# A sandwich of attention layers: transposing by halves of the array's rows

## The chip, the core and the metric

The kernel runs on one core of one Trainium2 chip. The metric is the time of one execution on the device in microseconds (us), the median of several runs. The core's engines work side by side, each through its own queue in order: PE (TensorE) multiplies matrices, PEld is PE's loading of the stationary operand, DVE (VectorE), ACT (ScalarE) and POOL (GpSimd) work elementwise, SP issues most of the DMAs. PE writes only to PSUM, which has eight banks of 512 float32 per partition here; ACT and DVE take its results from there to SBUF.

## The reference

The input x is 4 x 2048 x 256 in float32. First comes attention over all tokens, then two layers of local attention and feed-forward:

```python
x = x + _layernorm(_L0_attn_ref(_layernorm(x, axis=-1)), axis=-1)
x = x + _layernorm(_L0_ffn_ref(_layernorm(x, axis=-1), wqkv, q_scale, k_scale, wo, ln_g, ln_b, w1, b1, w2, b2), axis=-1)
```

`_L0_attn_ref` takes the scores x xᵀ, a softmax over their second axis and the product with x. One layer of `_L0_ffn_ref` (DEPTH = 2, 8 heads of 64, windows of 128 tokens) is

```python
h = shift_token(x); q, k, v = split(h @ wqkv)
q, k = rotary_xpos(l2norm(q) * qs, l2norm(k) * ksc)
o = local_attention(q, k, v)        # a window sees itself and the window before it, at most 128 tokens back
x = x + o @ wo
h = layernorm(shift_token(x)) * lg + lb
a, g = split(h @ w1 + b1)           # hidden width 682
x = x + (a * gelu(g)) @ w2 + b2
```

## The kernel before

Tokens lie on the partitions for row statistics and the residual stream, features lie there for products. Every operand of a product is kept in two float32r parts (`Split`: `hi`, the rounded value, and `lo`, the rest), and `products` (L149) makes three matmuls of each product: lo with hi, hi with lo, hi with hi. `split` (L132, L137) makes the parts from a PSUM bank: ACT copies it into `hi`, then DVE subtracts `hi` from the bank into `lo`. So each bank that is split stays taken until DVE has finished, and DVE waits for ACT.

The program has two phases. `global_phase` does the attention over all tokens for the four batch elements. `layer_phase` then walks over 128 steps (2 layers x 4 batch elements x 16 windows of 128 tokens). A step runs four generators in turns that are written out by hand in `TURNS`: `q` is `queries_keys` for the window two steps ahead, `s` the softmax of the next window, `v` (`outputs`) the attention output of this window, and `f` the feed-forward of two windows at a time. The order in which a generator's stages are called sets priorities; the framework's planner then orders the instructions of each engine by these and by its own estimate of when operands are ready, so neighbours on PE can come from different stages.

The places that the change touches, by the names under which the profile shows them:

- `queries_keys` makes q and k of a window in `qk` (tokens on the partitions, 16 heads x 64). After rotation (L616, L623, L645) and the scaling of k (L648) it transposes eight 128 x 128 blocks (L657): four of q into one bank `pqkT`, which is split into `qT`, then four of k into the next `pqkT`, split into `kT`.
- `similarities` takes the products `sim` of kT and qT. A head has 64 features, so the two heads of a pair use 64 of the array's 128 rows each, and write to two banks. DVE adds the mask and reduces (L702), ACT takes the exponential (L707), `pr` holds the weights, and POOL or ACT normalizes them (L720, L718).
- `weights(m)` transposes the weights of head pair m: four 128 x 128 blocks (two windows of keys x two heads; two blocks in a batch element's first window), L730, into one bank `pp`, which is split into `pT`.
- `values(m)` multiplies values and `pT` into `po`; two pairs share a bank, which is split into `oT`; `pw` is the product with wo. In the order of stages: weights(0), weights(1), values(0), weights(2), values(1), weights(3), values(2), and so on.
- The feed-forward has `phn` (transposes of the normalized rows), `pa` (first product) and `pf` (second product); `ph` are the transposes of h, `pv` the values, `pqk` the products for q and k.
- `BANKS` says how many banks each kind of PSUM tile has and which kinds share them: sim, pa, phn and pv share two; po and pw three; pf, ph and pqk one; pqkT one; pp one. `PLEFT` names those on the left side of PSUM, which come when the global phase gives up its big banks; the others come when that phase is over (`pools.more(2)`).
- `FIRST` orders the first steps of the layers into the end of the global phase: `q` and `r` are queries and keys of the first two windows, `c` a step of the global phase's ending, `s` the first window's softmax.

Steps that make a transpose are `nc.tensor.transpose(out, block, ident)`: the block is the stationary operand (PEld's row), the identity is what moves (PE's row, 128 columns).

Of the kernel before, what the change touches and what calls it, by code (L numbers as in the profile page):

```python
# [8 lines left out]
F32 = mybir.dt.float32  # L9
# [5 lines left out]
P = 128  # L15
HEADS = 8
DH = 64
# [11 lines left out]
BANKS = {'sim': (2, ('sim', 'pa', 'phn', 'pv')), 'po': (3, ('po', 'pw')), 't75': (1, ('pf', 'ph', 'pqk')), 't551': (1, ('pqkT',)), 't378': (1, ('pp', 'pb'))}  # L29
# [3 lines left out]
PLEFT = ('sim', 't75', 't551')  # L33
FIRST = 'qqccqrrccqrqqrccrrssss'
# [12 lines left out]
class Split:  # L47
    """A float32 operand in two float32r parts whose sum is exact: its upper 12 bits and the rest."""
# [9 lines left out]
def sandwich_kernel(  # L58
# [16 lines left out]
    """x += LN(attention over the batch's tokens of LN(x)); x += LN(two local-attention layers of LN(x)).  # L75

    First the attention over all tokens for each batch element, then each layer for all of them,
    with that layer's weights in SBUF. Tokens are on the partitions for the row statistics and the
    residual stream, features for the products, which are taken of operands in two parts each.
    """  # L80
    nc = tc.nc
# [3 lines left out]
    HID = w2.shape[1]  # L85
# [3 lines left out]
    NC = HID // P  # whole chunks of the hidden layer  # L89
    TAIL = HID - NC * P  # and the rest, the gate's at partition 64  # L90
    GT = 64
    # Where rows of the tail lie again: to, from, how many.
    PIECES = ((TAIL + 1, 0, GT - TAIL - 1), (GT + TAIL, GT - TAIL - 1, P - 1 - GT - TAIL))
    RING = 3  # windows whose keys and values are kept
# [6 lines left out]
    # ---------------------------------------------------------------- constants  # L101
# [8 lines left out]
    # Query i of a window sees keys i .. i + 128 of the previous and its own window: those of the  # L110
    # previous from i on, those of its own up to i. Here for the order previous, own, previous.
# [12 lines left out]
    # ---------------------------------------------------------------- operands in two parts  # L124
# [17 lines left out]
    def products(dst, terms, whole=()):  # L142
        """dst = the sum of the terms' lhsT.T @ rhs, with all of float32's bits, and of whole's as they are."""
        todo = []
        for a, b in terms:
            todo += [(a.lo, b.hi), (a.hi, b.lo), (a.hi, b.hi)]
        todo += whole
        for n, (a, b) in enumerate(todo):
            nc.tensor.matmul(dst, a, b, start=(n == 0), stop=(n == len(todo) - 1))  # L149

    # ---------------------------------------------------------------- row statistics
    def statistics(parts, n, name):
        """Mean and variance of n rows' parts, and 1/sqrt(variance + eps): [P, n, 2], [P, n]."""
# [18 lines left out]
    def normalize_all(dst, src, mv, rstd, engines, name):  # L172
        """Rows i of src, normalized, on the vector engine or the scalar engine."""
# [20 lines left out]
    def add_context(xg, y, b, g):  # L194
        """x + LN(y) goes to DRAM, and y becomes LN of that."""
# [10 lines left out]
    # ---------------------------------------------------------------- attention over all tokens  # L206
    JG = 2

    def global_phase(early, res, keep, big, bank):
        """Attention over all tokens.  # L210

        It stops before the last group's scores, when it's done with early, and after them, when
        it's done with res; the rest, in steps, uses only keep and bank.
        """
# [3 lines left out]
        def slot(tag, n, last):  # L218
            """The pool and the tag for the n-th of a kind of tiles; last are those that the last group uses."""
            n, last = n % GB[tag], [i % GB[tag] for i in last]  # L220
            return (res if n in last else early), f"{tag}{n}"

        def load_x(b, g):
            pool, tag = slot("x", b * NG + g, [B * NG - 1])
            t = pool.tile([P, 4, D], F32, tag=tag, bufs=1, name=f"x_{b}_{g}")
            # The first to come is waited for.
# [6 lines left out]
        def prepare(b, g):  # L233
            """LN(x) of 512 tokens with the features on the partitions."""
            xg = xt[b, g]
            mv, rstd = statistics([[xg[:, s, :]] for s in range(4)], 4, f"x_{b}_{g}")
            # |LN(x_j)|^2, the shift of column j's exponents: the exponents are 64 at most, one is 0.
# [21 lines left out]
        def scores(b, jg, hf):  # L259
            """exp of a half of the rows of JG chunks of scores."""  # L260
# [12 lines left out]
            for j in range(jg * JG, (jg + 1) * JG):  # L273
# [6 lines left out]
                # The scores are symmetric: those of the groups before are transposed here.  # L280
# [27 lines left out]
            for j in range(jg * JG, (jg + 1) * JG):  # L308
                # The sums belong to the contraction's index, so they divide LN(x).
# [14 lines left out]
        def context(b, jg, hf):  # L324
            """Adds the context of JG chunks; at the end x + LN(context) and LN of that go to DRAM."""
            for g in (2 * hf, 2 * hf + 1):
# [19 lines left out]
                if jg == NW // JG - 1:  # L346
                    if b + 1 < B:
                        add_context(early.tile([P, 4, D], F32, tag="xr", bufs=GB["xr"], name=f"xr_{b}_{g}"), y, b, g)
                    # The last one's rest is done when the first layer takes it.
# [37 lines left out]
    # ---------------------------------------------------------------- weights of a layer  # L387
# [5 lines left out]
    def tables(early, pool, l):  # L393
        """Rotation tables with the scales of q and k; the halves are swapped as the rotation does."""
# [29 lines left out]
    # The weights' parts, as they lie in SBUF.  # L424
# [11 lines left out]
    def split_weights(pool, bank, l):  # L436
        """Leaves layer l's weights in two parts in DRAM, piece by piece; each is left half a turn to arrive."""
        # The scale of the layer norm goes into w1, its shift into the bias.
# [34 lines left out]
        for i, (kind, ks, cols, src) in enumerate(pieces):  # L473
# [14 lines left out]
            # The lower part takes raw's place.  # L488
# [18 lines left out]
        # The tail's parts and the bias's, which meet rows of ones, share the rows of one product.  # L507
# [13 lines left out]
    def load_weights(pool, w, l, kinds):  # L521
        """Layer l's weights into w, as soon as the ones before aren't used any more."""
# [8 lines left out]
    # ---------------------------------------------------------------- the layers  # L531
    def layer_phase(pool, bank, ending):
# [22 lines left out]
        def features(l, b, u):  # L555
            """h of windows 2u and 2u + 1, features on the partitions: the second half comes one token late."""
# [21 lines left out]
        def queries_keys(l, b, w, n, wt, own):  # L578
            """Queries, keys and values of window w, left in own; in stages."""
# [19 lines left out]
            # Rotation, with the decay, the scales and, for q, the factor -8 in the tables; l2norm.  # L599
# [46 lines left out]
            # The similarities are scaled by q's.  # L646
# [6 lines left out]
            own["slot"] = n % RING  # L653
            for j, dst in enumerate((own["qT"], kT[:, n % RING])):
                pt = bank(f"pqkT_{at}_{j}")
                for c in range(4):
                    nc.tensor.transpose(  # L657
                        pt[:, c * P : (c + 1) * P],
                        qk[:, j * HEADS + 2 * c : j * HEADS + 2 * c + 2, :].rearrange("p h d -> p (h d)"),
                        ident,  # L660
                    )
                split(dst, pt.rearrange("p (c t) -> p c t", c=4))
                yield

        def local_attention(l, b, w, wt, before, own):
            """Window w sees itself and the window before it; y += its attention. In two streams of stages."""
# [5 lines left out]
            else:  # L672
# [3 lines left out]
                # In the order of their slots.  # L676
# [7 lines left out]
            def similarities(gq):  # L684
                # Negated similarities; the two heads of a pair use the two halves of the array's
                # rows, and so two banks.
# [37 lines left out]
            def weights(m):  # L724
                """The weights of pair m with the keys on the partitions."""
                pp = bank(f"pp_{at}_{m}").rearrange("p (f r t) -> p f r t", f=2, r=2)
# [330 lines left out]
```

## Time and profile before

| | |
|---|---|
| median of 3 runs | 3478.69 us (3476.59 to 3486.24) |
| profiled execution, span from first to last instruction | 3480.2 us |
| TensorE's mean granted clock | 0.991 |
| PE busy | 3374.0 us, 97% |
| PEld busy | 3069.6 us, 88% |
| DVE busy | 2932.9 us, 84% |
| ACT busy | 2495.6 us, 72% |
| POOL busy | 1933.8 us, 56% |
| transposes pp (L730) | 1984, busy 314.6 us |
| transposes pqkT (L657) | 1024, busy 158.9 us |
| similarities sim (L149) | 3 x 1024 matmuls of 64 rows, busy 788.2 us |

Of the profiled execution only the span is recorded; it stands 1.5 us from the median of the runs, so sums against the span and against the median are the same to 0.05%. PE's rows overlap: a matmul's row is longer than the time after which the next one starts, so PE's cost is read from the distance of starts, in PE's rows and above all in PEld's (a load that isn't held up starts when the matmul before it starts to stream). A row of the timeline that ends in x4 merges four instructions; its time runs from the first one's start to the last one's end.

### The profile page before, as it was taken

Reading aid. Unit: us, or ns where it says so; the run is one execution under the profiler, and the core shown is the slowest. Engines: PE = TensorE matmul, PEld = TensorE weight load, DVE = VectorE, ACT = ScalarE, POOL = GpSimd, SP = SyncE. Lnnn points to the kernel's source line nnn. Section 1 sums busy time; section 2 is a strip of 40 time slices with the busy share of each in tenths; the row PEclk is TensorE's granted clock in tenths of the full one; section 3 lists DMA queues with packets and bytes.
Section 4 is the critical chain, followed back from the end, with each engine's and each line's share of the span. In section 5 each row is a group of like instructions: output and inputs, shape, how many; then the busy total and the mean of one; then the engine's idle time right before and its main releaser. Section 6 shows DMA issues by size and latency. Waiting matters only on the chain.

```text
span 3480.2 us, 67843 instructions
## 1 busy us (share of the span) xinstructions
PE 3374.0 (97%) x24312; PEld 3069.6 (88%) x24312; DVE 2932.9 (84%) x7549; ACT 2495.6 (72%) x5826; POOL 1933.8 (56%) x1975
## 2 busy tenths in 40 slices
PE   8999999999999999999999999999999999999997
PEld 7989999978889999999888898888888888888886
DVE  6797877778888888888999888888888888888886
ACT  5556655467777888777777777777777777777774
POOL 3234313265556666666666655666666666566562
PEclk9999999999999999999999999999999999999998
DMA  3243312110000000001111112101000010011001
GB/s 98 93 145 116 127 47 92 63 65 22 23 23 25 24 25 23 23 25 34 36 35 35 49 59 68 29 29 30 29 29 29 29 31 25 26 30 30 29 22 30
DMA packets 158194, 156.70 MB, mean 45 GB/s; under 512 B 27466, under 2 KB 145056, under 8 KB 157344
## 3 DMA queue, kind: packets, MB, share of 16 engines
q1 hardware_dynamic: 157856, 152.36, 14.1%
q8 instruction: 192, 3.15, 0.4%
q14 instruction: 146, 1.20, 0.1%
HBM read 86.39 MB, written 54.79 MB: 41 GB/s over the span
## 4 chain that ended last, share of the span: by engine, by line
PE 79%; DVE 11%; ACT 5%; DMA 2%; issue 2%; POOL 1%; SPq 0%; POOLq 0%; ACTq 0%; DVEq 0%
PE pa L149 12%; PE sim L149 10%; PE po L149 9%; PE pqk L149 9%; PE c L149 8%; PE pf L149 6%; PE pp L730 6%; PE pv L149 5%; PE pw L149 5%; PE s L149 5%; PE pqkT L657 3%; DVE pr L702 2%; DVE hn L168 1%; DVE y L168 1%; DVE qk L648 1%
## 5 line engine op out<-in xcount | busy, mean ns | idle before, releaser
L720 POOL TENSOR_SCALAR pr<-pr,rr 128x256 f32<-128x256 f32 (+1 forms) x768 | 356.1, 481 | 650.9 <-DVE rr L713 494.2
L707 ACT ACTIVATE pr<-pr,nm 128x256 f32<-128x256 f32 (+1 forms) x1024 | 507.8, 498 | 123.4 <-DVE nm L702 118.5
L702 DVE CUSTOM_DVE_ANT_0 pr<-sim,mask,rn 128x256 f32<-128x256 f32 (+1 forms) x1024 | 440.1, 470 | 92.3 <-PE sim L149 88.5
L149 PE MATMUL pa<-hnT_h,w_l 128*128 128x256 f32 x1408 | 407.1, 289 | 3.5 <-DVE hnT_l L137 2.2
L630 POOL TENSOR_TENSOR rn<-ss,neghalf 128x16 f32<-128x16 f32 x128 | 394.1, 3079 | 27.7 <-DVE ss L610 20.0
L616 POOL TENSOR_TENSOR sw<-qk,ab 128x512 f32<-128x512 f32 x256 | 338.3, 1322 | 115.2 <-ACT qk L596 115.2
L149 PE MATMUL pa<-hnT_l,w_h 128*128 128x256 f32 x1408 | 398.8, 283 | 0.3 <-DVE hnT_l L137 0.2
L149 PE MATMUL pa<-hnT_h,w_h 128*128 128x256 f32 x1408 | 399.0, 283 | 0.0
L137 DVE TENSOR_TENSOR pT_l<-pp,pT_h 128x512 fp32r<-128x512 f32 (+1 forms) x512 | 340.0, 664 | 27.7 <-ACT pT_h L132 23.4
L623 POOL TENSOR_TENSOR qk<-qk,ab 128x512 f32<-128x512 f32 x256 | 349.4, 1377 | 10.2 <-ACT sq L602 9.0
L132 ACT CAST pT_h<-pp 128x512 fp32r<-128x512 f32 (+1 forms) x512 | 291.7, 570 | 68.2 <-PE pp L730 62.8
L149 PE MATMUL po<-pT_l,v_h 128*128 128x256 f32 x992 | 316.3, 319 | 4.6 <-DVE pT_l L137 4.6
L730 PE MATMUL pp<-ident,pr 128*128 128x128 f32 x1984 | 314.6, 276 | 3.7 <-DVE pT_l L137 1.7
L149 PE MATMUL po<-pT_h,v_l 128*128 128x256 f32 x992 | 298.2, 301 | 2.6 <-ACT pT_h L132 2.4
L132 ACT CAST act_h<-af 128x256 fp32r<-128x256 f32 x320 | 130.2, 407 | 237.2 <-DVE af L833 233.9
L149 PE MATMUL sim<-kT_h,qT_l 64*128 64x256 f32 (+1 forms) x1024 | 294.0, 329 | 0.9 <-ACT kT_h L132 0.6
L149 PE MATMUL c<-xs_h,e_l 128*128 128x256 f32 x1024 | 285.3, 285 | 3.6 <-ACT y L132 2.5
L149 PE MATMUL c<-xs_l,e_h 128*128 128x256 f32 x1024 | 287.5, 283 | 0.8 <-POOL xs_l L137 0.8
L149 PE MATMUL c<-xs_h,e_h 128*128 128x256 f32 x1024 | 287.5, 283 | 0.0
L149 PE MATMUL po<-pT_h,v_h 128*128 128x256 f32 x992 | 278.9, 281 | 0.0
L149 PEld LDWEIGHTS pa<-hnT_h,w_l 128*128 128x128 f32 x1408 | 269.4, 191 | 5.6 <-DVE hnT_l L137 2.7
L149 PEld LDWEIGHTS pa<-hnT_l,w_h 128*128 128x128 f32 x1408 | 269.5, 191 | 1.1 <-DVE hnT_l L137 1.0
(179 smaller groups left out, 11841.3 us busy)
## 6 DMA issues: line engine op xcount, KB each, us to landing
yd<-y SPq DMA_DIRECT2D x32, 512.0 KB
y<-yd SPq DMA_DIRECT2D x32, 512.0 KB
ab<-abd SPq DMA_DIRECT2D x128, 128.0 KB
x<-in_L_attn_x_dram SPq DMA_DIRECT2D x15, 512.0 KB
x<-x1d SPq DMA_DIRECT2D x15, 512.0 KB
out_dram<-y SPq DMA_DIRECT2D x15, 512.0 KB
h<-y SPq DMA_DIRECT2D x64, 112.0 KB
xr<-in_L_attn_x_dram SPq DMA_DIRECT2D x12, 512.0 KB
```

The lines of the kernel that those rows point to most:

```text
L132: (nc.scalar.copy if eng == "a" else nc.vector.tensor_copy if eng == "v" else nc.gpsimd.tensor_copy)(dst, src)
L137: eng.tensor_tensor(dst.lo, src, dst.hi.bitcast(F32), ALU.subtract)
L149: nc.tensor.matmul(dst, a, b, start=(n == 0), stop=(n == len(todo) - 1))
L168: nc.vector.tensor_scalar(dst, src, mv[:, i, 0:1], rstd[:, i : i + 1], ALU.subtract, ALU.mult)
L616: nc.gpsimd.tensor_mul(sw4[:, hs], qk4[:, hs, ::-1, :], ab[:, 1, j].unsqueeze(1).to_broadcast([P, HEADS, 2, DH // 2]),)
L623: (nc.vector if T1[j] == "v" else nc.gpsimd).tensor_mul(qk[:, hs, :], qk[:, hs, :], ab[:, 0, j].rearrange("p h i -> p (h i)").unsqueeze(1) ...
L630: nc.gpsimd.tensor_tensor(rn, ss, neghalf, ALU.pow)
L657: nc.tensor.transpose(pt[:, c * P : (c + 1) * P], qk[:, j * HEADS + 2 * c : j * HEADS + 2 * c + 2, :].rearrange("p h d -> p (h d)"), ident,)
L702: nc.vector.tensor_tensor_reduce(out=pr[:, r, 0:NK], in0=sim, in1=mask[:, m0 : m0 + NK], scalar=3.0e38, scale=own["rn"][:, h : h + 1] if Q ...
L707: nc.scalar.activation(pr[:, r, 0:NK], pr[:, r, 0:NK], AF.Exp, bias=nms[h], scale=-1.0, accum_out=rs[:, h : h + 1],)
L720: (nc.gpsimd if e == "p" else nc.vector).tensor_scalar(pr, pr, rr[:, h : h + 1], 1.0, ALU.mult, ALU.mult)
L730: nc.tensor.transpose(pp[:, f, r, :], prs[m][:, r, f * P : (f + 1) * P], ident)
```

## The change

Each transpose of pp and pqkT is made in two: rows 0 to 63 of the block (tokens or queries) on the upper half of the array's rows, rows 64 to 127 on the lower half, each 64 x 128 with a 64 x 64 piece of the identity, each into its own PSUM bank. The tile for this, `tt`, has two banks, there is one of it, and pqkT and pp share it. So it takes eight blocks at once: q and k of a window together, and two pairs of weights together (`weights(gq)`). The number and size of the splits stay; each reads both banks and puts the halves together. weights(0) now makes pairs 0 and 1, weights(1) pairs 2 and 3, after values(0). The other banks move: po and pw have two instead of three, pqk, ph and pf have two instead of one and take pv with them, sim keeps two without pv. sim now lies on the right side of PSUM, so the first window's softmax comes after the global phase's last step in the program's order (it stood after the last `c` before, too). The comments are also gone.

```diff
-BANKS = {'sim': (2, ('sim', 'pa', 'phn', 'pv')), 'po': (3, ('po', 'pw')), 't75': (1, ('pf', 'ph', 'pqk')), 't551': (1, ('pqkT',)), 't378': (1, ('pp', 'pb'))}
+BANKS = {'sim': (2, ('sim', 'pa', 'phn')), 'po': (2, ('po', 'pw')), 't75': (2, ('pf', 'ph', 'pqk', 'pv')), 'tt': (1, ('pqkT', 'pp'))}
-PLEFT = ('sim', 't75', 't551')
-FIRST = 'qqccqrrccqrqqrccrrssss'
+PLEFT = ('t75', 'tt')
+FIRST = 'qqccqrrccqrqqrccrr'
...
+    HT = P // 2
+    def transpose_halves(dst, c, src):
+        for h in range(2):
+            rows_ = slice(h * HT, (h + 1) * HT)
+            nc.tensor.transpose(dst[:, h, c, :], src[rows_], ident[rows_, rows_])
+    def parts(a, f):
+        return Split(f(a.hi), f(a.lo))
...
+            pt = bank(f"pqkT_{at}").rearrange("p (h c t) -> p h c t", h=2, c=8)
+            for c in range(8):
+                transpose_halves(pt, c, qk[:, 2 * c : 2 * c + 2, :].rearrange("p h d -> p (h d)"))
             for j, dst in enumerate((own["qT"], kT[:, n % RING])):
-                pt = bank(f"pqkT_{at}_{j}")
-                for c in range(4):
-                    nc.tensor.transpose(
-                        pt[:, c * P : (c + 1) * P],
-                        qk[:, j * HEADS + 2 * c : j * HEADS + 2 * c + 2, :].rearrange("p h d -> p (h d)"),
-                        ident,
-                    )
-                split(dst, pt.rearrange("p (c t) -> p c t", c=4))
+                src = pt[:, :, 4 * j : 4 * j + 4].rearrange("p h c t -> p c h t")
+                split(parts(dst, lambda t: t.rearrange("p c (h t) -> p c h t", h=2)), src)
                 yield
...
-            def weights(m):
-                pp = bank(f"pp_{at}_{m}").rearrange("p (f r t) -> p f r t", f=2, r=2)
-                pT = split_pool(pool, [P, 2, 2, P], "pT", BUFS["pT"], f"pT_{at}_{m}")
-                for f in range(nh):
-                    for r in range(2):
-                        nc.tensor.transpose(pp[:, f, r, :], prs[m][:, r, f * P : (f + 1) * P], ident)
-                split(pT[:, 0:nh], pp[:, 0:nh])
-                return pT
+            def weights(gq):
+                pp = bank(f"pp_{at}_{gq}").rearrange("p (h c t) -> p h c t", h=2, c=8)
+                out = []
+                for c in range(2):
+                    for f in range(nh):
+                        for r in range(2):
+                            transpose_halves(pp, (c * 2 + f) * 2 + r, prs[2 * gq + c][:, r, f * P : (f + 1) * P])
+                for c in range(2):
+                    m = 2 * gq + c
+                    pT = split_pool(pool, [P, 2, 2, P], "pT", BUFS["pT"], f"pT_{at}_{m}")
+                    out.append(pT)
+                    src = pp[:, :, 4 * c : 4 * c + 2 * nh].rearrange("p h c t -> p c h t")
+                    split(parts(pT, lambda t: t[:, 0:nh].rearrange("p f r (h t) -> p (f r) h t", h=2)), src)
+                return out
...
-                pTs = [weights(0)]
+                pTs = weights(0)
                 yield
-                pTs.append(weights(1))
                 yield
...
+                        if m == 0:
+                            pTs += weights(1)
                         if m < 2:
-                            pTs.append(weights(m + 2))
                             yield
...
         pools.more(2)
+        for _ in attention(0)[0]:
+            pass
...
-                    return self.ps[tag not in PLEFT].tile([P, 512], F32, tag=tag, bufs=bufs, name=name)
+                    size = 1024 if tag == "tt" else 512
+                    return self.ps[tag not in PLEFT].tile([P, size], F32, tag=tag, bufs=bufs, name=name)
```

More of the change, by code (lines that the diff above doesn't have):

```diff
@@ L915, in layer_phase @@
         load_weights(pool, wts[0], 0, "kv")
-        first = [start(0), None, None]
+        first = [start(0), None]
         for w in range(BUFS["ab"]):
@@ L926, in layer_phase @@
                 continue
-            i = "qrs".index(t)
+            i = "qr".index(t)
             if first[i] is None:
-                first[i] = start(1) if i == 1 else attention(0)[0]
+                first[i] = start(1)
             next(first[i], None)
```

## The prediction

> **What bounds the kernel now.** I read the page's busy shares and the chain that ended last first, then the groups of the transposes, then the timeline of PE's weight loads (PEld), whose starts show what a matmul really costs.
>
> ```profile
> PE 3374.0 (97%) x24312; PEld 3069.6 (88%) x24312; DVE 2932.9 (84%) x7549; ACT 2495.6 (72%) x5826; POOL 1933.8 (56%) x1975
> PE 79%; DVE 11%; ACT 5%; DMA 2%; issue 2%; POOL 1%; SPq 0%; POOLq 0%; ACTq 0%; DVEq 0%
> ```
> ```profile
> L730 PE MATMUL pp<-ident,pr 128*128 128x128 f32 x1984 | 314.6, 276 | 3.7 <-DVE pT_l L137 1.7 <-DVE rr L713 0.9 <-POOL qk L623 0.7
> L657 PE MATMUL pqkT<-ident,qk 128*128 128x128 f32 x1024 | 158.9, 277 | 10.4 <-DVE qk L645 6.3 <-DVE kT_l L137 2.0 <-DVE qk L648 1.7
> ```
>
> PE is the bound: it is busy almost throughout and makes 79% of the chain. The layers take some 2780 us of the span (about 700 to 3480) in 128 steps, 21.7 us a step. In each there are 24 transposes, 16 of pp and 8 of pqkT, and PE hardly waits for them (3.7 and 10.4 us in the whole run): their banks pp and pqkT are in time today.
>
> PEld around a batch of transposes, two of sim, and their neighbours:
>
> ```profile
> 1501.35 0.47 PEld L730 LDWEIGHTS pp<-ident,pr 128*128 128x128 f32 x4
> 1501.79 0.19 PEld L149 LDWEIGHTS po<-pT_l,v_h 128*128 128x128 f32 x1
> ...
> 1502.14 0.19 PEld L149 LDWEIGHTS po<-pT_l,v_h 128*128 128x128 f32 x1
> 1502.26 0.19 PEld L149 LDWEIGHTS po<-pT_h,v_h 128*128 128x128 f32 x1
> 1502.58 0.18 PEld L149 LDWEIGHTS sim<-kT_h,qT_l 64*128 64x128 f32 x1
> 1502.69 0.19 PEld L149 LDWEIGHTS sim<-kT_l,qT_h 64*128 64x128 f32 x1
> 1502.80 0.19 PEld L149 LDWEIGHTS sim<-kT_h,qT_h 64*128 64x128 f32 x1
> 1502.92 0.19 PEld L149 LDWEIGHTS sim<-kT_h,qT_l 64*128 64x128 f32 x2
> ...
> 1503.51 0.19 PEld L149 LDWEIGHTS sim<-kT_h,qT_h 64*128 64x128 f32 x1
> 1503.83 0.19 PEld L149 LDWEIGHTS pqk<-wq_h,hT_l 128*128 128x128 f32 x1
> ```
>
> Three things are to be seen. Four transposes go by from 1501.35 to 1501.79: 0.11 each. The x2 rows are two loads at once, for the two heads of a pair on the two halves of the rows: two halves do run side by side. And between a matmul on 128 rows and one on 64 the loads stand 0.32 apart (1502.26 to 1502.58, and back 1503.51 to 1503.83), where neighbours of one kind stand 0.12 apart: **each change between whole and half rows costs 0.20 us**, in which nothing is loaded ahead. I followed all changes after 760 us in the timeline: 746 of them, and in none does the next load start less than 0.198 us after the last matmul's start; between matmuls of one kind it starts with it.
>
> What bounds a transpose, load or stream? These are the loads of pqkT in a place where PE had stood idle, read in windows that end after one, two and three of them:
>
> ```profile
> 1766.47 0.14 PEld L657 LDWEIGHTS pqkT<-ident,qk 128*128 128x128 f32 x1 [0.68 <-issue]
> ...
> 1766.47 0.20 PEld L657 LDWEIGHTS pqkT<-ident,qk 128*128 128x128 f32 x2 [0.68 <-issue]
> ...
> 1766.47 0.31 PEld L657 LDWEIGHTS pqkT<-ident,qk 128*128 128x128 f32 x3 [0.68 <-issue]
> ```
>
> A row lasts 0.14, so the second load starts 0.06 after the first (0.20 - 0.14): the load itself takes 0.06. The third starts 0.11 after the second: it waits for the first block to stream. So streaming 128 columns is the limit, 0.109 to 0.11 us; the load needs about half of that.
>
> **The change, part by part.** *Halves on PE.* A half streams 64 columns, by proportion 0.055 us (an estimate from the 0.109), and still loads 128 columns, 0.06. Two halves side by side then take about 0.06 instead of 0.11. Bounds: 0.055 if the load hides better, 0.11 if it doesn't shorten; without any overlap two halves take 0.12. I take 0.06, since the loads that I can see overlap (x2) are on just these half rows.
>
> *The drains.* Sims are on half rows already, the transposes were on whole rows, and now change sides. Take a batch of eight blocks, from the last load before it to the first load after. Before: 0.12 + 8 x 0.109 = 0.99 us. After: 0.32 to the first half's load, 8 pairs at 0.06 = 0.47, then 0.20 for the drain: 0.99. **The drains eat the whole gain**: 24 x 0.05 = 1.2 us a step is saved, and three batches a step x two changes x 0.20 = 1.2 us is paid. Over 128 steps 150 us stand against 150.
>
> The Trainium skill's page "TensorEngine Tiling (Array Packing)", section Tiling Modes, warns that changing the tiling mode drains the TensorE. It gives no price; the 0.20 above is the trace's.
>
> The page "TensorE: Matmul & The Clock Gate", section LDWEIGHTS, has a load take its columns divided by 1.2, so 107 ns for 128 columns whatever the rows. That fits sim (1502.58 to 1502.69), but not the 0.06 of these float32 transposes. By the page a batch would come to 0.32 + 8 x 0.107 + 0.20 = 1.38, and the run to 0.39 x 384 = 150 us more, about 3630.
>
> *Neighbours.* A batch that touches a sim saves both changes there, 0.40 us. The timeline has 170 such contacts of pp or pqkT with sim from 760 us on, 1.4 a step, for six batches of four; with three of eight I take 0.8 a step: 0.3 us a step, 41 us gained (bounds 0 and 1.4 x 0.40 x 128 = 72).
>
> *Batches torn apart.* All eight blocks of pqkT share a tile now, but k is ready later than q: L648 ends 5.5 us after q's transposes start, on average over the steps. If the planner puts other work between the two, each step has one more batch, 0.40 us or 51 in all; if k is ready by the time the tile is free, nothing. I take 26.
>
> *The shared tile.* This is the wait that takes the place of stream time. Today's use of one bank, from the timeline:
>
> ```profile
> 1501.46 0.60 PE L730 MATMUL pp<-ident,pr 128*128 128x128 f32 x4
> ...
> 1502.91 0.57 ACT L132 CAST pT_h<-pp 128x512 fp32r<-128x512 f32 x1
> ...
> 1504.00 0.69 DVE L137 TENSOR_TENSOR pT_l<-pp,pT_h 128x512 fp32r<-128x512 f32 x1
> ```
>
> From the first transpose to DVE's end it is 3.2 us here; over all uses that I could pair the mean is 3.24 for pp and 2.89 for pqkT. pp's bank is taken 4 x 3.24 = 13.0 us of 21.7, pqkT's 5.8. Now one tile carries all three batches, each with two splits one after the other: 0.7 on PE, then twice 0.58 wait, 0.57 cast, 0.83 wait, 0.67 subtraction (means of the same uses), 6.0 us. Three make 18 of 21.7 us, plus waits for k. That leaves little, and PE is in order: a transpose that waits holds back the values, products and feed-forward queued behind it. Bounds: 0, if the plan spaces the batches well, and 2 us a step, if k's wait (up to 5.5) comes on top of the 18 (23.7). I take 0.5 us a step, 64 us.
>
> *The other banks* (one answer): sim's two lose pv, which takes 18.7 us of late loads off pv and helps phn (35.8 us late now, by the timeline); po's loss of a bank may cost as much. Zero, bounds -40 and +40. The splits read the same 512 columns in runs of 64; rows with broken patterns (L648, 0.69) are as long as plain ones (L645, 0.68): zero. The first softmax: sim's first load is at 694.40 already, after the last c at 693.00: zero, -1 to +3.
>
> Sum: 0 - 41 + 26 + 64 = +49 us. From 3478.69 (the span, 3480.2, stands 1.5 us above; only the span is recorded) that is 3528; **I forecast 3530 us**, 1.5% slower.
>
> **The rivals.** *Faster.* The batches lean on sims as often as now (-72), and sim's banks are freer (-40 at most; I take half, -20), with no wait on the tile: 3390 to 3420. For it: DVE and ACT have room, and the planner reorders freely. Against: nothing in the order of turns was laid out for a tile that is held 18 us of 21.7. It decides where the tile's waits stay under 0.5 us a step.
>
> *No overlap.* If the two transposes of a pair go one after the other, a batch takes 0.32 + 16 x 0.06 + 0.20 = 1.46 instead of 0.99, over 384 batches 180 us: 3660. For it: no transpose runs on half rows in this trace. Against: sim's x2 rows.
>
> *The tile as the bound.* With k's wait on top, the step goes to 23.7 us: 2 x 128 = 256 us, 3735.
>
> *The change doesn't do what it says*, halving nothing: the stream of 64 columns takes as long as 128. That is the 3630 of a pair at 0.11.
>
> **How the numbers follow.** The forecast's mechanism (drains against streams, tile waits of a few tenths) gets 0.50, its own range 3490 to 3610; faster 0.27; no overlap or no halving, 3620 to 3670, 0.12; the tile as the bound 0.06; terms that cancel within 0.3%, 0.05. About 0.3%, 10 us, is what a measurement of this kernel can tell from no change. The range, 3395 to 3670, leaves out the tile as the bound and the ends of the others. Faster 0.27, same 0.05, slower 0.68.
>
> **What would show it.** In PEld: rows of pp and pqkT in pairs, pairs 0.06 apart; 0.32 between them and whole-row neighbours; more changes of rows, from 6 a step to about 10 to 12. In the waits: PE or PEld at pp or pqkT held by DVE's pT_l, qT_l or kT_l, far above today's few us. Pairs 0.11 or 0.12 apart would refute the halving; drains that vanish, or a tile that never holds PE, would make it faster.

## The result, and the profile after

The changed kernel takes 3907.65 us (median of 4 runs, 3904.96 to 3911.22) against 3481.27 us (median of 4 runs of the kernel before): a ratio of 1.1224, 95% interval 1.1208 to 1.1240. It is 426 us slower, where 49 us were forecast. The profiled execution spans 3904.1 us at a mean granted clock of 0.925 (before: 3480.2 us, 0.991).

The page of the changed kernel: span, busy shares, granted clock in 40 slices, and the chain that ended last by engine.

```profile
span 3904.1 us, 73785 instructions
PE 3522.7 (90%) x27320; PEld 3100.3 (79%) x27320; DVE 3003.5 (77%) x7549; ACT 2527.8 (65%) x5826; POOL 1909.3 (49%) x1975
PEclk9999999899989998899999988889989988989898
PE 56%; DVE 26%; ACT 9%; DMA 3%; issue 3%; POOL 2%; SPq 0%; POOLq 0%; DVEq 0%; ACTq 0%
```

The span and the clock's row of the kernel before:

```profile
span 3480.2 us, 67843 instructions
PEclk9999999999999999999999999999999999999998
```

No engine has become the bound: every share of the span fell, PE's from 97% to 90%, and PE makes 56% of the chain where it made 79%. DVE went from 11% to 26% of it. But for the last slice, the slices with an 8 in the clock's row are new.

PEld at a batch of transposes, in the timeline of the changed kernel:

```profile
1502.56 0.19 PEld L149 LDWEIGHTS pw<-wo_l,oT_h 128*128 128x128 f32 x1
1502.68 0.19 PEld L149 LDWEIGHTS pw<-wo_h,oT_h 128*128 128x128 f32 x1
1503.00 0.45 PEld L158 LDWEIGHTS pp<-ident,pr 64*128 64x128 f32 x12
1503.52 0.19 PEld L149 LDWEIGHTS pa<-hnT_h,w_l 128*128 128x128 f32 x1
```

The change does what it says: twelve loads, six pairs, lie between 1503.00 and 1503.45. One load's row lasts 0.14 (median of all), so the last starts at 1503.31, five pairs after the first: 0.06 a pair. The step from whole rows to the halves is 0.32 (1502.68 to 1503.00).

PE's waits in the changed kernel: in all, times, the longest, us.

```profile
PE po L149 <- DVE pT_l L137: 150.5, 98, 5.8
PE po L149 <- ACT pT_h L132: 71.4, 59, 2.6
```

The same two before:

```profile
PE po L149 <- DVE pT_l L137: 4.6, 3, 2.4
PE po L149 <- ACT pT_h L132: 2.4, 5, 0.8
```

This is where PE waits most: the product po waits for the split of the weights just transposed, 222 us against 7. The tile itself holds PE for little (pp waits for DVE's pT_l for 12.5 us, 26 times).

One batch's splits in the changed kernel, both pairs out of one tile:

```profile
1505.68 0.58 ACT L132 CAST pT_h<-pp 128x512 fp32r<-128x512 f32 x1
1506.29 0.69 DVE L137 TENSOR_TENSOR pT_l<-pp,pT_h 128x512 fp32r<-128x512 f32 x1
1507.02 0.59 ACT L132 CAST pT_h<-pp 128x512 fp32r<-128x512 f32 x1 [0.27 <-DVE pT_l L137]
1507.63 0.69 DVE L137 TENSOR_TENSOR pT_l<-pp,pT_h 128x512 fp32r<-128x512 f32 x1 [0.32 <-ACT pT_h L132]
```

The second cast waits for the first subtraction, though it reads other columns. Over all batches that I could pair, the tile is held 6.8 us for weights and 5.4 us for q and k, and stands free for 2.0 us between uses. A step takes (3904 - 707) / 128 = 25.0 us, and the tile is held for 2 x 6.8 + 5.4 = 19.0 of them. The free time is what the holds leave of a step, so that the two add up to it (19.0 + 3 x 2.0 = 25.0) says nothing of what bounds the step. Before, pp's own bank stood free about as long between uses: (21.7 - 13.0) / 4 = 2.2 us.

PE's rows at a window that starves, again the changed kernel:

```profile
1537.07 0.71 PE L158 MATMUL pp<-ident,pr 64*128 64x64 f32 x16
...
1538.18 0.28 PE L149 MATMUL po<-pT_l,v_h 128*128 128x256 f32 x1
1538.29 0.28 PE L149 MATMUL po<-pT_h,v_h 128*128 128x256 f32 x1
1540.44 0.38 PE L149 MATMUL po<-pT_h,v_l 128*128 128x256 f32 x1 [1.87 <-ACT pT_h L132]
1541.83 1.11 PE L826 MATMUL phn<-ident,hn 128*128 128x128 f32 x4 [1.00 <-ACT hn L193]
1543.40 0.58 PE L149 MATMUL po<-pT_l,v_h 128*128 128x256 f32 x1 [0.47 <-DVE pT_l L137]
1543.78 0.41 PE L149 MATMUL po<-pT_h,v_h 128*128 128x256 f32 x1
1544.00 0.41 PE L149 MATMUL po<-pT_h,v_l 128*128 128x256 f32 x1
```

Up to 1538.29 po's neighbours start 0.11 to 0.12 apart; after five microseconds with hardly any work they start 0.21 apart (1543.78 to 1544.00): the clock is at half. The granted clock stands there for 586 us of the changed kernel's span, against 61 before.

I made one count for all kernels, against before, from their timelines. **Gaps**: time by which PE's starts stand further apart than the matmul's stream, where they are over 0.5 us apart, after 760 us. **Clock**: time over the full clock's stream in stretches at half clock, where the starts stand about a doubled stream apart, after 707 us. **Changes** of rows: 0.20 us each, after 760 us. **Streams**: 24 transposes x 0.049 us x 128 steps = 150 us saved where all are halved. For the changed kernel: gaps 406 - 82 = +325, clock 129 - 15 = +114, changes 1390 - 746 = 644, +129, streams -150: +418, and the spans differ by 424.

### The profile page after: what moved, and what is told of

The parts are those of the page before. It is cut to its first block, busy times and chain, and to the rows that moved or that the text cites. A ratio compares the mean times of both kernels' runs of the same rounds, so it can differ in the third digit from the quotient of the medians.

```text
span 3904.1 us, 73785 instructions
## 1 busy us (share of the span) xinstructions
PE 3522.7 (90%) x27320; PEld 3100.3 (79%) x27320; DVE 3003.5 (77%) x7549; ACT 2527.8 (65%) x5826; POOL 1909.3 (49%) x1975
## 4 chain that ended last, share of the span: by engine, by line
PE 56%; DVE 26%; ACT 9%; DMA 3%; issue 3%; POOL 2%; SPq 0%; POOLq 0%; DVEq 0%; ACTq 0%
PE pa L149 14%; PE c L149 8%; PE po L149 6%; PE pf L149 5%; DVE pr L711 4%; PE s L149 4%; ACT pr L716 4%; PE sim L149 3%; PE pw L149 3%; DVE ss L621 3%; DVE hn L180 3%; DVE pT_l L137 3%; PE pqk L149 3%; PE pp L158 2%; PE pv L149 2%
## 5 line engine op out<-in xcount | busy, mean ns | idle before, releaser
L149 PE MATMUL pa<-hnT_h,w_l 128*128 128x256 f32 x1408 | 438.9, 312 | 18.4 <-ACT hnT_h L132 10.0
L149 PE MATMUL pa<-hnT_l,w_h 128*128 128x256 f32 x1408 | 421.1, 299 | 4.0 <-DVE hnT_l L137 3.8
L149 PE MATMUL po<-pT_h,v_l 128*128 128x256 f32 x992 | 325.9, 328 | 72.3 <-ACT pT_h L132 71.4
L149 PEld LDWEIGHTS po<-pT_l,v_h 128*128 128x128 f32 x992 | 211.8, 213 | 196.8 <-DVE pT_l L137 184.3
L149 PEld LDWEIGHTS pa<-hnT_h,w_l 128*128 128x128 f32 x1408 | 292.6, 208 | 34.4 <-ACT hnT_h L132 12.5
L149 PE MATMUL po<-pT_h,v_h 128*128 128x256 f32 x992 | 307.6, 310 | 0.0
L848 DVE SCALAR_TENSOR_TENSOR af<-pa,b1c,ge 128x256 f32<-128x256 f32 x320 | 154.3, 482 | 190.4 <-ACT ge L846 188.8
L149 PEld LDWEIGHTS pa<-hnT_l,w_h 128*128 128x128 f32 x1408 | 291.5, 207 | 7.9 <-DVE hnT_l L137 5.9
L149 PEld LDWEIGHTS po<-pT_h,v_l 128*128 128x128 f32 x992 | 210.4, 212 | 102.6 <-ACT pT_h L132 88.1
L149 PEld LDWEIGHTS pa<-hnT_h,w_h 128*128 128x128 f32 x1408 | 290.5, 206 | 0.0
```

The costliest lines, as they stand in the source:

```text
L848: nc.vector.scalar_tensor_tensor(af, pa[:, 0, :], b_[:, c : c + 1], ge, ALU.add, ALU.mult)
```

## The experiments

Medians; ratios are to the kernel before, run on the same chip. "Whole rows" means transposes as before. The last columns are the count's terms against before.

| run | median us | ratio [95%] | gaps | clock | changes |
|---|---|---|---|---|---|
| changed kernel | 3907.65 | 1.1224 [1.1208, 1.1240] | +325 | +114 | +129 |
| e1 whole rows, shared tile | 3818.65 | 1.0965 [1.0949, 1.0981] | +267 | +92 | -12 |
| e2 casts first | 3836.49 | 1.1021 [1.1002, 1.1039] | +288 | +93 | +150 |
| e3 weights halved, by eight | 3612.97 | 1.0372 [1.0356, 1.0387] | +59 | +27 | +160 |
| e4 two po banks | 3486.62 | 1.0014 [1.0005, 1.0023] | +9 | -1 | -3 |
| e5 pair per bank | 3819.12 | 1.0970 [1.0954, 1.0987] | +273 | +88 | -12 |
| e6 weights halved, by four | 3541.14 | 1.0172 [1.0155, 1.0189] | +1 | +2 | +176 |
| e7 weights whole, by eight | 3516.19 | 1.0101 [1.0084, 1.0119] | +34 | +1 | -14 |
| e9 q and k apart | 3907.76 | 1.1243 [1.1220, 1.1266] | +330 | +108 | -2 |
| e10 regrouped banks alone | 3776.43 | 1.0862 [1.0844, 1.0880] | +261 | +75 | -28 |
| e11 e10, two tiles shared | 3701.51 | 1.0643 [1.0626, 1.0660] | +201 | +60 | -18 |
| e13 e10, one product bank | 3521.07 | 1.0123 [1.0104, 1.0143] | +100 | +2 | -36 |
| e14 before, two product banks | 3832.84 | 1.1017 [1.0993, 1.1040] | +222 | +93 | -3 |
| e15 changed, one product bank | 3769.61 | 1.0844 [1.0817, 1.0871] | +273 | +57 | +120 |
| e16 e1, one product bank | 3742.09 | 1.0743 [1.0710, 1.0775] | +230 | +43 | -9 |
| e17 e11, one product bank | 3689.86 | 1.0594 [1.0576, 1.0611] | +171 | +38 | +12 |
| e18 e17, three po banks | 3699.94 | 1.0619 [1.0603, 1.0635] | +184 | +35 | +14 |

With streams taken off (150 us, or 16 x 0.049 x 128 = 100 where only the weights are halved) the terms come within 39 us of the difference of the spans, the largest miss at e14 (312 against 351). So the count leaves no large term of the slow kernels unnamed; for the small differences it is too coarse (e13: 66 against 38).

**The halves alone, in the order of before.** e4 takes away po's third bank, e6 halves the weights too, still four blocks at a time, in a two-bank tile of their own:

```diff
-'po': (3, ('po', 'pw'))
+'po': (2, ('po', 'pw'))
-nc.tensor.transpose(pp[:, f, r, :], prs[m][:, r, f * P : (f + 1) * P], ident)   # e6
+transpose_halves(pp, f * 2 + r, prs[m][:, r, f * P : (f + 1) * P])
```

> The kernel before with two banks for po and pw instead of three, and nothing else: the price of that part of the new bank plan, and the control for kernels that take a bank from po. Theories T and D: 3470 to 3500 us, no change that can be told. A third theory, that the smaller groups of banks are what costs (theory B): over 3550 us.

> The kernel before with the weights' transposes in halves, four blocks at a time as before (the stages keep their order), in a two-bank tile of their own half filled, po with two banks. Nothing is shared and no batch is larger; only halves and drains are new. Theory T with my drain sum: a batch of four costs 0.32 + 0.24 + 0.15 = 0.71 us instead of 0.56, four batches, 128 steps: +77 us, less where sims are neighbours; 3520 to 3570 us. Theory D (halves and drains are the loss): over 3650 us.

e4 is 3486.62, so po's third bank is worth 5 us. e6 is 55 us above e4: 896 more changes at 0.20 make 179, and 16 x 0.049 x 128 = 100 is saved, 79. Halving without a shared tile behaves as its streams and drains say; gaps and clock stay as they were.

e3 and e7 transpose the weights by eight, as the change does, in a two-bank tile of their own; e3 in halves, e7 in whole rows:

```diff
-pp = bank(f"pp_{at}_{m}")          # [P, 512], weights(m)
+pp = bank(f"pp_{at}_{gq}")         # [P, 1024], weights(gq), two pairs, then their splits
+transpose_halves(...)              # e3;  nc.tensor.transpose(..., ident) in e7
```

> The kernel before with only the weights' transposes in halves, eight blocks at a time, in a two-bank tile of their own; q and k stay whole in their own bank, po has two banks instead of three. Theory T: the weights hold their tile 2 x 6.8 us of a step and nobody else wants it; 3500 to 3650 us. Theory D: two thirds of the loss stays, as two of three batches keep their drains; 3720 to 3800 us.

> The kernel before with the weights transposed whole, but eight blocks at a time into a two-bank tile of their own, both splits on both banks, po with two banks: the control for the weights in halves in a tile of their own (3613 us). Theory T (batches of eight in a tile held longer, without sharing, cost a part): 3500 to 3580 us, and the rest up to 3613 is halves and drains. If batches of eight are free: 3480 to 3495 us.

By eight costs 30 us over e4 (3516 against 3487), halves on top 97 (3613). Both are far from 426.

**Inside the changed kernel.** e1 keeps its bank plan, its shared tile and its batches, but transposes whole rows; blocks alternate between the two banks, so each split still reads both. e5 is e1 with each pair in one bank.

```diff
-transpose_halves(pp, (c * 2 + f) * 2 + r, prs[2 * gq + c][:, r, f * P : (f + 1) * P])
+nc.tensor.transpose(pp[:, r, c * 2 + f, :], prs[2 * gq + c][:, r, f * P : (f + 1) * P], ident)   # e1
+nc.tensor.transpose(pp[:, c, f, r, :], ..., ident)                                             # e5
```

> The changed kernel with its banks and its shared two-bank tile as they are, but each transpose whole again on 128 rows; the blocks of a batch alternate between the tile's two banks, so that both splits still read both banks. If the time is lost to the shared tile (theory T): about as slow as the changed kernel, 3850 to 3950 us, with PE waiting at po for pT as there. If it is lost to the halves and their drains (theory D, changes between whole and half rows, 0.2 us each): back to 3490 to 3560 us.

> The changed kernel's bank plan and shared tile with whole transposes, as in the kernel of whole rows in the same tile (3819 us), but one pair of weights (and q or k) to a bank, so that the two splits of a batch read different banks and the second pair's cast need not wait for the first pair's subtraction. Theory T (the tile is held too long): half a microsecond to a microsecond less of each hold, 3700 to 3790 us. If the splits' order on the banks doesn't matter and only the sharing by q, k and weights does: 3800 to 3830 us.

e1 is 3818.65: without any halves 337 of the 426 us remain, and the halves make 89. It lies between the ranges of its two theories, so each explains a part. e5 is the same as e1 (3819.12). It doesn't decide what it was meant to: in its trace the second pair's cast still follows the first pair's subtraction, so the turns go by tile and the banks can't be told apart by it.

e2 lets both casts of a batch go before both subtractions:

```diff
-for c in range(2): split(...)                 # cast, subtraction, cast, subtraction
+for c in range(2): nc.scalar.copy(dst.hi, src)
+for dst, src in todo: nc.vector.tensor_tensor(dst.lo, src, dst.hi.bitcast(F32), ALU.subtract)
```

> The changed kernel, but of a batch of weights both casts come before both subtractions, so the second pair's cast no longer waits for the first pair's subtraction on the same banks (223 us of ACT's idle time there in the changed kernel). Theory T: the tile is held some 1 us less per batch of weights and pair 1 or 3 comes earlier, pair 0 or 2 later; 3780 to 3890 us. Theory D: no change, 3895 to 3920 us.

71 us come back (3836.49): the weights hold the tile for 5.8 us instead of 6.8, while q and k hold it for 7.3 instead of 5.4. The turns in the tile are a part, not the bulk.

e9 is e1 with q and k in two batches of four out of the shared tile, so that q doesn't wait for k:

```diff
-pt = bank(f"pqkT_{at}")                 # eight blocks of q and k
+pt = bank(f"pqkT_{at}_{j}")             # four blocks, for j in (q, k)
```

> Whole rows in the changed kernel's shared two-bank tile (3819 us), but q and k come one after the other in two batches of four, as before the change, so that no use of the tile waits for k with q already in it. If joining q and k in one batch is what costs: back to 3520 to 3620 us. If it is the ring of uses of one tile (each held 6 us for weights, some 3 for q or k, and 2 us from its release to the next use): a use more a step, 2 x 6.2 + 2 x 2.9 + 4 x 1.9 = 26 us a step at worst, not faster than 3760 and up to 4000 us.

It is slower than e1 (3907.76 against 3818.65): the join of q and k isn't the bulk of the cost. In e1 the two together hold the tile 5.8 us, in e9 each alone 2.5 us, and a fourth use a step, with its own time between uses, costs more than the wait for k.

**The other banks.** e10 makes only the changed kernel's grouping of the other banks; pqkT and pp have one bank each and are transposed as before. e14 goes the other way: the kernel before, with a second bank for pqk, ph and pf, while pv stays with sim (for this pqkT lies on the right side of PSUM, and the last first-step stages come after the global phase).

```diff
-BANKS = {'sim': (2, ('sim', 'pa', 'phn', 'pv')), 'po': (3, ...), 't75': (1, ('pf', 'ph', 'pqk')), ...}
+BANKS = {'sim': (2, ('sim', 'pa', 'phn')), 'po': (2, ...), 't75': (2, ('pf', 'ph', 'pqk', 'pv')), ...}     # e10
+BANKS = {'sim': (2, ('sim', 'pa', 'phn', 'pv')), 'po': (2, ...), 't75': (2, ('pf', 'ph', 'pqk')), ...}     # e14
```

> The changed kernel's grouping of all other banks (two for pqk, ph, pf and pv; two for sim, pa and phn; two for po; softmax of the first window after the global phase), but transposes as before: whole, by four, pqkT and pp with a bank each. If the ring of the shared tile is the loss: 3470 to 3510 us. If the grouping is: over 3700 us.

> The kernel before with two banks for pqk, ph and pf, two for po (as in the changed kernel), but pv still among sim's banks; to fit, pqkT lies on the right side, and the last stages of the first two windows come after the global phase (some 10 us at most). Theory L: the products for q and k run ahead as in the regrouped kernels, those for v don't; 3550 to 3750 us. Theory V: 3470 to 3510 us.

This is the find: e10 is 3776.43, so the grouping that I had put at zero is 290 us slower than e4 with no transpose touched. e14 is 346 us slower than e4 with a second product bank as its main edit, and slower than the range of theory L, which it supports. e13 puts that bank back to one in e10, and e15 does so in the changed kernel:

```diff
-'t75': (2, ('pf', 'ph', 'pqk', 'pv'))
+'t75': (1, ('pf', 'ph', 'pqk', 'pv'))
```

> The kernel with regrouped banks (3776 us), but one bank instead of two for pqk, ph, pf and pv; one bank stays empty. In the regrouped kernels the products for q and k start 84 us and those for v 69 us ahead of the end of their window, in the kernel before 69 and 48. If the second bank lets PE run these products ahead and leaves it without work in the chain of a window (theory L): 3490 to 3580 us, with leads near those of before. If it is that pv no longer holds sim's banks (theory V): 3700 us or more.

> The changed kernel as it is, but with one bank instead of two for pqk, ph, pf and pv. Theory L: the run-ahead goes and some 300 us with it, what stays is the shared tile and the halves; 3600 to 3720 us, with the granted clock over 0.97. Theory V: 3880 to 3930 us.

e13 is 3521.07: taking a bank away, and leaving it empty, makes the kernel 255 us faster than e10. The pages of e10 and e13 have the same instructions on PE:

```profile
PE 3450.7 (92%) x24312; PEld 3111.7 (83%) x24312; DVE 2970.1 (79%) x7549; ACT 2516.9 (67%) x5826; POOL 1928.7 (51%) x1975
```
```profile
PE 3323.5 (94%) x24312; PEld 3014.0 (86%) x24312; DVE 2904.6 (83%) x7549; ACT 2514.5 (71%) x5826; POOL 1940.8 (55%) x1975
```

What differs is their order, and the bank that some of them write to. With two banks the planner lets PE make q, k and v earlier: from the start of a window's product for v (pv) to its last pw it is 69 us in e10 and 50 in e13 (before: 48). PE's waits at the weights' transposes and at po, first in e10, then in e13:

```profile
PE po L149 <- ACT pT_h L132: 62.9, 46, 2.8
PE pp L742 <- DVE pT_l L137: 56.5, 74, 3.9
```
```profile
PE pp L742 <- DVE pT_l L137: 43.1, 48, 1.9
PE po L149 <- ACT pT_h L132: 6.5, 10, 1.5
```

My reading then was that PE spends its filler work early and has none left when a window's chain of transposes, splits and po comes. In the changed kernel one bank brings back only 138 us (e15: 3769.61, above the 3600 to 3720 that theory L gave), so the shared tile costs by itself too. Three last kernels took that apart: e16 is e1 with one product bank, e17 and e18 are e13 with pqkT and pp sharing two one-bank tiles instead of having one each (po with two banks and with three); e11 is e17 with two product banks.

```diff
-'t551': (1, ('pqkT',)), 't378': (1, ('pp',))
+'tt': (2, ('pqkT', 'pp'))              # e11, e17, e18: four blocks each, whole rows
```

> As the kernel with regrouped banks, but pqkT and pp share two one-bank tiles, whichever is free: the same two banks that the changed kernel joins into one tile, shared by the same users. If it is sharing that costs: 3700 us or more. If it is that one tile lets in one batch at a time: 3450 to 3520 us, as a batch can be transposed while another is split.

> The changed kernel's shared tile, with whole-row transposes and one bank (not two) for pqk, ph, pf and pv; so the changed kernel less the halves and less the second bank. Theory (the second bank's run-ahead, the shared tile and the halves are three separate costs): the tile holds three batches of about 6 us a step here too, so PE waits for it, but less starved: between the kernel with one bank each and whole rows (3521) and the one with halves (3770); the halves cost 55 to 97 us in calm order, so 3670 to 3720. Rival (once the second bank is gone the shared tile is free of charge and the halves make all of the remaining 249 us): 3510 to 3560.

> The regrouped banks with one bank for pqk, ph, pf and pv; q, k and the weights in whole rows by four, but sharing two tiles of one bank each instead of one each; po two banks. Theory (a transposed batch that finds a second tile no longer holds PE; with two banks of products ahead this brought 75 us): 3440 to 3500, against 3521 with one tile each. Rival (in the calm order PE waits for the weights themselves and not for their tile): 3505 to 3530.

> As the kernel with two shared one-bank tiles and one bank for pqk, ph, pf and pv, with po back at three banks, all eight banks in use. Theory (po's third bank is worth 6 us, as it was in the kernel before): within 10 us of the kernel with two po banks, 3430 to 3500. Rival (a third bank lets PE run ahead as the second bank of the products did): over 3530.

e16 is 3742.09. With one product bank the shared tile costs 221 us over e13 and the halves only 28 more (e15). Both expectations missed: the one had the tile too cheap, the other had it free. e11, where the second tile had brought 75 us over e10, had been taken to show that a second tile helps. e17 refutes that: against e13 the same edit costs 169 us (3689.86). And its lead is hardly longer than e13's (from pv to the last pw 51 us, against 50), so running ahead isn't needed for the loss. e18's third po bank changes it by 10 us; it lies over 3530, as its rival had it, but only because e17 does. PE's waits in e17:

```profile
PE phn L823 <- DVE hn L180: 38.8, 41, 1.7
PE pw L149 <- DVE oT_l L137: 33.6, 34, 3.2
```

They stand elsewhere than in the changed kernel: of e17's gaps 26 us end at po, of the changed kernel's 252. What all the slow orders share is gaps of PE, and half clock behind them. None of the kernels beats the one before.

**Idle time and clock.** e8 and e12 add 3072 matmuls that nothing uses, six ahead of each pair's values, to the changed kernel and to the kernel before: 3072 x 0.119 = 366 us at full clock.

```diff
+for k in range(6):
+    nc.tensor.matmul(po[:, m % 2]..., wt["o"].hi[:, k % 4, 0:P], wt["o"].hi[:, (k + 1) % 4, :], start=True, stop=True)
 products(...)
```

> The changed kernel with six more matmuls (wo's parts, 256 columns, results overwritten) ahead of each pair's values, 3072 in all, 366 us at full clock. If PE idles in waits and the half clock follows the idle time: they fall into idle time and raise the granted clock from 0.925 to over 0.95; the time rises by 0 to 150 us (3900 to 4060). If PE is the bound, or the clock has another cause: 4230 us or more, with the clock near 0.92.

> The kernel before with the same 3072 extra matmuls as the changed kernel got (366 us at full clock; the changed kernel took them for 166 us): the control. PE is the bound here, so nearly all shows: 3780 to 3860 us, clock 0.99.

In the changed kernel 366 us of work cost 167 us (4074.26, ratio 1.1705 [1.1681, 1.1728]): the mean clock rises from 0.925 to 0.963, the half-clock time falls from 586 to 307 us, and the gaps shrink from 406 to 300. In the kernel before they cost 296 us (3774.04 against 3477.97 in the same round, ratio 1.0851 [1.0829, 1.0873]) with the clock at 0.992. Both results stand just outside their ranges, by 14 and 6 us. The signs are as expected: idle time and the clock hang together, and the PE of before has much less to give.

## Why the prediction was wrong

**Right: the halves.** A pair goes by in 0.06 us, so the rival of no overlap and that of no halving are refuted. The entering drain is 0.32 between loads. Changes rose from 6 to about 11 a step, as said (1390 after 760 us). Drains and streams come to +129 - 150 = -21 us, against 0 - 41 + 26 = -15 in the sum. In experiments the halves cost 28 (e15 over e16), 55 (e6 over e4), 89 (changed over e1) and 97 us (e3 over e7). Where the weights alone are halved it is mostly drains (in e6 over e4 and e3 over e7 the changes come to 179 and 174 us, against 100 saved); where all 24 transposes are, drains and streams nearly cancel, and it is gaps and clock. One sum on the way is off: 0.32 + 16 x 0.06 + 0.20 is 1.48, not 1.46, so the rival of no overlap stood at 3667 and not 3660; nothing else rests on it.

**Wrong: "The other banks (one answer): ... Zero, bounds -40 and +40".** In e10 this step alone costs 290 us over e4. It was priced by which tile loses or gains a bank. In this framework a bank is also an input of the planner, and with it the planner laid out another order on PE for the whole of the layers (69 us from pv to the last pw in e10, 48 before). Putting one product bank back, nothing else, takes 255 of the 290 away (e13). pv's move and the rest of the grouping are worth 35.

**Wrong in place and size: the shared tile, 0.5 us a step, 64 us.** The 18 us that it is held were right (2 x 6.8 + 5.4 = 19.0). The wait was put at the transposes, which would hold back what is queued behind them; there PE waits 12.5 us in the whole run. It waits at po instead, 222 us, for splits of which the second pair's follows the first's. The size depends on the plan: 42 us with two product banks (e1 over e10), 221 with one (e16 over e13), so the terms don't add. The rival "the tile as the bound" came nearest to the time, but its cause was k's wait, and e9 speaks against that. Whether the 2.0 us between uses belong to the cost isn't shown.

**Missing: the clock.** The sum took full clock throughout. The stretches at half clock cost 114 us more than before by the count, and they follow the gaps.

**Shown and not shown.** Shown is that the loss is gaps and clock (the count), that the grouping alone costs 290 us and the shared tile with whole rows, without the second product bank, 221, that a second product bank suffices for a loss of this size (e10 and e13; e14 with small further edits), and that a second tile for the transposes brings 169 (e17 and e13). Argued only is that the order makes the gaps, and how the planner comes to these orders: no run keeps the order and changes the banks alone. Running ahead goes with two product banks (from the first product for q and k to the last pw 88 us in the changed kernel, 69 before), but e17 has the loss without it. Why more room makes a worse order stays open.

## What to carry to other kernels

Where a planner orders the engines by its own estimates, a change of buffer counts changes the order of everything: price it by building the regrouping alone before the change that needs it, and don't count a free bank as harmless. A PE at 97% has little slack, so waits added to the chain behind it show as gaps, and many of them show a second time as a slower clock (e13: 100 us more of gaps, 2 of clock; the changed kernel: 325 and 114). Two halves side by side pay only where many of them stand between two changes of rows, and where their tile doesn't tie together batches that were apart: here four pairs lose (e6, 55 us), and in the changed kernel eight gain 21 us by the count, which gaps and clock more than take back.

## What the runs showed of the hardware

**Half clock comes from mostly idle windows.** After 760 us the changed kernel has 71 stretches at half clock, each a multiple of 3.413 us (up to 17.07; the last is cut off near the program's end) on one grid that holds through the run. In the 3.413 us ahead of such a stretch PE starts 9 matmuls (median, from 0 to 23), and the longest distance between two starts is 1.84 us (median; 0.96 in the least idle one). So no gap as long as the window is needed. In the kernel before there are 12 such stretches.

How much of a window PE streams tells the two kinds of window nearly apart; this is an estimate from the timelines. Taking 0.055, 0.109, 0.119 and 0.232 us for the streams of 64, 128, 256 and 512 columns, and the windows of the grid at full clock, the streams fill at most 0.43 of each of the 69 windows that half clock follows in the changed kernel, and at least 0.41 of each of the 682 others; before it is at most 0.36 in 10 and at least 0.40 in 768. In all the traces of this case together, no window filled less than 0.36 was followed by full clock; some filled up to 0.60 were followed by half clock, but 95% of those that were lie under 0.43.

The Trainium skill's page "TensorE: Matmul & The Clock Gate", Part 1 (The HAM clock gate), has the clock fall to half after an idle window of about 3.4 us. The length agrees with the 3.413 us here; the same part also tells of a kernel in which frequent short idles between groups of matmuls were enough, and these runs agree with that, with the numbers above.

**Leaving half rows is cheaper after short streams.** From the start of the last 64-column transpose of a batch to the next load on whole rows it is 0.150 us, where 0.20 was taken from the sims' 256 columns. Entering after 256 columns takes 0.207 from start to load, as before, and after 512 columns 0.319, in both kernels: the time grows with the stream of the last matmul.

**Readers of one tile take turns.** In e1 and in e5, with the pair's blocks over both banks or in one, the second cast on ACT starts only after DVE's first subtraction, in all 256 batches, and the kernels' medians agree within 0.5 us. That is the order the framework gives; what the banks themselves would do isn't shown.
